# The V slice of a graph-attention layer: two score blocks side by side, and another order of its fifteen products

## The chip, the cores and the metric

The kernel runs on one NeuronCore of a Trainium2 chip. Times are device microseconds of that core: the median of several runs for a verdict, and one profiled execution for everything that is read out of a trace. TensorE is called PE here, and its weight loads PEld; VectorE is DVE, ScalarE is ACT, GpSimd is POOL, SyncE is SP, which only issues transfers. PE writes its results to PSUM; DVE and ACT read them from there; POOL works on SBUF alone.

## The reference, cut to what matters

One layer of masked attention over a graph, with a normalisation and a ReLU ahead of it. `x` is 128 graphs x 128 nodes x 768 features, `adj` 128 x 128 x 128, twelve heads of 64, all in float32.

```python
h = jnp.maximum(_layernorm(x, axis=-1), 0.0)
q = _split_heads(h @ Wq + bq)
k = _split_heads(h @ Wk + bk)
v = _split_heads(h @ Wv + bv)
scores = jnp.einsum('bhqd,bhkd->bhqk', q, k) / jnp.sqrt(HD)
scores = scores + beta * adj_e
scores = jnp.where(adj_e > 0, scores, -9000000000000000.0)
out = jnp.einsum('bhqk,bhkd->bhqd', jax.nn.softmax(scores, axis=-1), v)
x = x + out.transpose(0, 2, 1, 3).reshape(x.shape)
```

## The kernel before, in words

Four graphs make a group `G`; there are 32 groups. Group 0 takes a plain path; groups 1 to 31 run three slices each: `qk0` (Q and K of the first half of the heads), `v` (V of all heads) and `qk1` (Q and K of the second half).

**Products.** In a slice the multiplication of the activations by the weights is done with fifteen products in place of eighteen, at two levels of a scheme of Strassen's kind (`PRODUCTS`, with sums of operands made beforehand). A product (`product_z`, line 531) is 14 matmuls in seven zones, 28 rows in a trace, since each float32 matmul stands there twice, with a weight load each. Each product belongs to one of four chains, `a` to `d`. A chain owns a pair of PSUM banks, from its first product in the slice to its last, and its products add up there: after each product the sum so far is read out and added to or subtracted from one of six results (`uses`), and only then may the chain's next product write to the pair. So the next product of a chain waits for the reading of the one before. In the V slice a first reading of a result is a DVE instruction (line 561, with the bias) and then an ACT instruction (line 562); each later one is one DVE addition (line 571).

**Order.** The tuple `ORDER[slice]` gives the order of the products. A place in it is called a slot here. What stands at slots 0 to 14 of the V slice, with the chain of each, is `1a 0c 3b 5a 2c 7b 10a 6c 11b 13a 4d 9c 14b 8d 12c`. `run` (line 807) issues, for each slot, the matmuls of the product, then what is listed behind it (`behind_product`, line 797: masks of score blocks from the slot before, then the `todo` of this slot, then what fell due), then the readings of this product, then the trailing ACT work, then the `"post"` entries. `then(n, f, ...)` enters `f` at slot `n`. All engines carry out what they are given in that order; nothing is moved by a scheduler after that (`manual_schedule`).

**Score blocks.** `scores(G, u, j)` (line 617) takes a pair of PSUM banks and issues 16 matmuls on 64 x 64 tiles of the array (32 rows of line 626), where products and the weighting with V use 128 x 64 tiles. Then it gives back two of the eight homes (SBUF tiles in which the results of slices lie), those of (0, j) and (1, j); the first reading of a later result takes the home that has been free longest. At the next slot DVE adds the mask (line 634), which frees the PSUM pair, and ACT takes the exponential (line 636). Three score blocks of a group stand in its V slice (u = 0: j = 2 at slot 0, j = 1 at slot 2, j = 0 at slot 7), three in the `qk0` slice of the next group.

**PSUM.** There are four pairs, handed round in the order in which they were given back. In the V slice chains a, c and b hold three, and the fourth goes to a score block, then to chain d, which starts at slot 10.

**Decoding.** When the last product of a result has been read, POOL turns its zones into plain Q, K or V (`decode`, line 581: lines 589 to 592 for Q and K, 600 to 604 for V). A score block needs the decoded results of its columns.

**Other work in the V slice.** For the group after next, ACT takes the statistics of four rows of x in three instructions each (`row_stats`, lines 417 to 419) at posts 1, 5 and 10, and SP loads the next row (line 409) at posts 2 and 6. For the next group ACT normalises x (`norm`, line 446) at posts 3, 4, 7 and 8, two instructions each; DVE transposes it; POOL makes inner sums (lines 469 to 471). DVE adds the results of the attention of the group before (line 708). Weights of a product that are not resident are loaded by SP into a ring of five tiles (`load_T`, line 335), each as soon as a buffer is free.

## Time and profile before

| what | value |
| --- | --- |
| median of three runs | 2707.47 us (2703.18 to 2716.2) |
| the profiled execution's own time | 2712.82 us |
| span of its trace | 2711.0 us |
| granted PE clock, mean | 0.996 |
| PE busy | 99% of the span |
| DVE, POOL, ACT busy | 81%, 77%, 65% |

A matmul's end is modelled in the trace, and one starts while the one before still runs. So the busy share of PE says little, and what counts is when the first matmul of a product starts and when the first of the next one does. A row of the timeline has its start and its length in us, the engine, the line, what it writes and reads, and how many instructions were merged; in square brackets is the idle time of the engine ahead of it and what ended that. A row of the table of waits has the waiting engine and line, what it waited for, and the total, the number and the longest of these waits.

### The profile page before, as it was taken

To read this page: it belongs to the slowest core of one execution; us is meant where nothing else is said; L and a number is where in the kernel's file an instruction comes from. 1 tells how busy PE (TensorE), PEld (TensorE's weight loads), DVE (VectorE), ACT (ScalarE), POOL (GpSimd) and SP (SyncE) were. 2 spreads that over 40 slices of the span, in tenths; PEclk is the share of its full clock that TensorE was granted. 3 is DMA by queue.
4 is the path that set the end of the run, shared out by engine and by line. 5 is a ranking of instruction groups with operands and counts; after the bars stand their busy time and mean duration, and the time that the engine had idled before them with its cause. 6 is when DMAs were issued, how large, how long until landed. Compare 5 with 4: busy or idle time off the path is not lost.

```text
span 2711.0 us, 121562 instructions
## 1 busy us (share of the span) xinstructions
PE 2674.2 (99%) x52029; PEld 2568.3 (95%) x52029; DVE 2188.4 (81%) x2705; ACT 1762.5 (65%) x4612; POOL 2096.0 (77%) x3034
## 2 busy tenths in 40 slices
PE   8999999999999999999999999999999999999997
PEld 7799999999999999999999999999999999999997
DVE  6878888788888788888788878788887888877885
ACT  2476666677666677666767666776666776667653
POOL 4867878777878877888778787778787778887783
PEclk9999999999999999999999999999999999999999
DMA  8789889899889898889899889898898988888875
GB/s 229 262 260 278 274 271 274 259 281 276 271 264 281 260 287 272 271 278 277 259 277 276 275 274 268 269 273 269 270 283 260 280 272 269 280 269 256 253 235 158
DMA packets 530342, 721.73 MB, mean 266 GB/s; under 512 B 105980, under 2 KB 374024, under 8 KB 529800
## 3 DMA queue, kind: packets, MB, share of 16 engines
q1 hardware_dynamic: 528640, 713.12, 86.4%
q8 instruction: 412, 6.75, 1.0%
q10 hardware_dynamic: 1160, 0.79, 0.1%
q14 instruction: 130, 1.06, 0.1%
HBM read 647.73 MB, written 66.05 MB: 263 GB/s over the span
## 4 chain that ended last, share of the span: by engine, by line
PE 87%; POOL 4%; DVE 3%; ACT 2%; DMA 1%; issue 1%; POOLq 0%; DVEq 0%; ACTq 0%
PE pair L547 74%; PE pair L626 7%; PE pair L683 6%; DMA sbig<-in_x_dram 1%; DVE home L571 1%; POOL home L590 1%; POOL home L589 1%; POOL home L592 1%; ACT sbig L419 0%; POOL home L591 0%; ACT sbig L417 0%; ACT home L562 0%; DVE e L634 0%; DVE prep_v L304 0%; ACT e L636 0%
## 5 line engine op out<-in xcount | busy, mean ns | idle before, releaser
L571 DVE TENSOR_TENSOR home<-home,pair 128x896 f32<-128x896 f32 x810 | 860.2, 1075 | 234.2 <-PE pair L547 130.4
L547 PE MATMUL pair<-sbig,T_qk 128*64 128x128 f32 x13888 | 888.6, 274 | 4.1 <-ACT e L666 3.1
L547 PEld LDWEIGHTS pair<-sbig,T_qk 128*64 128x64 f32 x13888 | 758.0, 137 | 17.8 <-issue 8.0
L666 ACT ACTIVATE e<-e,sm 128x64 f32<-128x64 f32 x1512 | 382.2, 341 | 123.5 <-DVE sm L654 123.2
L547 PE MATMUL pair<-A,T_qk 128*64 128x128 f32 x6076 | 415.1, 273 | 0.0
L547 PE MATMUL pair<-T_v,sbig 128*64 128x128 f32 x6944 | 414.2, 274 | 0.3 <-ACT home L562 0.3
L589 POOL TENSOR_TENSOR home<-home 128x256 f32<-128x256 f32 x297 | 227.2, 765 | 237.0 <-DVE home L571 237.0
L683 PE MATMUL pair<-v,e 128*64 128x65 f32 x6048 | 401.8, 221 | 0.0
L565 ACT ACTIVATE home<-pair 128x640 f32<-128x640 f32 x325 | 229.2, 705 | 261.5 <-PE pair L547 196.8
L547 PEld LDWEIGHTS pair<-T_v,sbig 128*64 128x64 f32 x6944 | 385.4, 137 | 6.3 <-issue 4.3
L683 PEld LDWEIGHTS pair<-v,e 128*64 128x64 f32 x6048 | 359.5, 137 | 3.6 <-DVE e L634 0.3
L547 PEld LDWEIGHTS pair<-A,T_qk 128*64 128x64 f32 x6076 | 331.7, 137 | 5.5 <-issue 5.5
L634 DVE SCALAR_TENSOR_TENSOR e<-pair,biasT 128x1024 f32<-128x1024 f32 x189 | 230.4, 1219 | 82.1 <-PE pair L626 82.0
L592 POOL TENSOR_TENSOR home<-home 128x256 f32<-128x256 f32 x297 | 276.3, 930 | 23.3
L590 POOL TENSOR_TENSOR home<-home 128x256 f32<-128x256 f32 x297 | 250.1, 842 | 23.3
L636 ACT ACTIVATE e<-e 128x1024 f32<-128x1024 f32 x189 | 200.2, 1059 | 64.7 <-DVE e L634 56.7
L446 ACT ACTIVATE x<-x,block 128x192 f32<-128x192 f32 x480 | 231.7, 540 | 0.0
L692 ACT ACTIVATE sm<-pair,tiny 128x8 f32<-128x8 f32 x189 | 49.3, 261 | 261.6 <-PE pair L683 261.6
L591 POOL TENSOR_TENSOR home<-home 128x128 f32<-128x128 f32 x297 | 196.9, 663 | 23.3
L547 PE MATMUL pair<-sbig,res_qk 128*64 128x128 f32 x3472 | 211.9, 273 | 0.0
L567 ACT ACTIVATE home<-pair,bqk 128x128 f32<-128x128 f32 x650 | 203.6, 374 | 0.0
L626 PE MATMUL pair<-home 64*64 64x128 f32 x5312 | 196.2, 277 | 6.3 <-issue 4.8
(192 smaller groups left out, 4699.9 us busy)
## 6 DMA issues: line engine op xcount, KB each, us to landing
T_qk<-kept_qk SPq DMA_DIRECT2D x713, 448.0 KB, 4.8
T_v<-kept_v SPq DMA_DIRECT2D x341, 448.0 KB, 4.9
xo<-in_x_dram SPq DMA_DIRECT2D x189, 256.0 KB, 4.5
out_dram<-xo SPq DMA_DIRECT2D x189, 256.0 KB, 5.9
x<-in_x_dram SPq DMA_DIRECT2D x248, 192.0 KB, 6.6
sbig<-in_x_dram SPq DMA_DIRECT2D x116, 384.0 KB, 6.5
kept_qk<-prep_qk SPq DMA_DIRECT2D x23, 448.0 KB, 2.9
adj<-in_adj_dram SPq DMA_DIRECT2D x128, 64.0 KB, 3.9
```

The lines of the kernel that those rows point to most:

```text
L446: nc.scalar.activation(t, t, AF.Relu, bias=shift[G, n], scale=rstd[G, n])
L547: nc.tensor.matmul(p[q:q + HD, at, :], lhs[:, q:q + HD], rhs, start=(first and at % 4 == 0), stop=True, skip_group_check=True)
L565: nc.scalar.activation(t[:, 0:5], p[:, 0:5], AF.Copy, scale=float(sign))
L567: nc.scalar.activation(t[:, at], p[:, at], AF.Identity, bias=bqk[:, of, oc:oc + 1], scale=float(sign))
L571: nc.vector.tensor_tensor(t, t, p[:, 0:7], op)
L589: e.tensor_tensor(t[:, 1:4:2], t[:, 1:4:2], twice(5), ALU.add)
L590: e.tensor_tensor(t[:, 2:5:2], t[:, 2:5:2], twice(1), ALU.add)
L592: e.tensor_tensor(t[:, 0:7:6], t[:, 0:7:6], twice(2), ALU.add)
L626: nc.tensor.matmul(ps[k:k + HD, i, g * N:(g + 1) * N], keys[r, k:k + HD], queries[r], start=True, stop=True)
L634: nc.vector.scalar_tensor_tensor(e, ps, SCORE_CAP * ISCALE, bias, op0=ALU.min, op1=ALU.add)
L666: nc.scalar.activation(o[:, r, b, 0:HD], pa[:, r, b, 0:HD], AF.Copy, scale=t[:, 1, r, b:b + 1])
L683: nc.tensor.matmul(pa[q:q + HD, 2 * g + i, :], k[:, q:q + HD], vt[G, "v", r, h // 4][:, 4 * g + h % 4, :], start=True, stop=True, skip_gro ...
```

## The change

The V slice gets an order of its own, the score block of j = 2 moves from slot 0 to slot 2, ahead of that of j = 1, and two of the four normalisations move one slot up. The order of slots 0 to 14 becomes `1a 0c 5a 2c 3b 10a 7b 6c 13a 11b 4d 9c 14b 8d 12c`; slots 10 to 14 are as before. `row_stats` and the loads of rows keep their slots. The slots whose weights are resident stay the same (1, 5, 10 and 14 of the V slice), but other products stand there.

```diff
-ORDER = {"qk0": ZORDER, "v": ZORDER, "qk1": QORDER}
+PORDER = (1, 0, 5, 2, 3, 10, 7, 6, 13, 11, 4, 9, 14, 8, 12)
+ORDER = {"qk0": ZORDER, "v": PORDER, "qk1": QORDER}
...
         todo.clear()
-        then(0, scores, G, 0, 2)
+        then(2, scores, G, 0, 2)
         then(2, scores, G, 0, 1)
         then(7, scores, G, 0, 0)
         if more:
             then((11, "post"), add_raw, G + 1)
-            for n, at in enumerate((3, 4, 7, 8)):
+            for n, at in enumerate((3, 4, 6, 7)):
                 then((at, "post"), norm, G + 1, 2 + n // 2, n % 2 * 2, n % 2 * 2 + 2)
```

## The prediction

> **What bounds the kernel now.** I read the page first, then the waits, then PE's timeline in V slices with and without stops.

> ```profile
> span 2711.0 us, 121562 instructions
> PE 2674.2 (99%) x52029; PEld 2568.3 (95%) x52029; DVE 2188.4 (81%) x2705; ACT 1762.5 (65%) x4612; POOL 2096.0 (77%) x3034
> ```

> PE bounds it: idle time is 36.8 us of 2711.0. A change that leaves its matmuls alone can gain in two ways only: fewer costs between matmuls, which the trace counts as busy, or fewer stops. Both are seen in the V slice of group 28, here PE alone.

> ```profile
> 2382.79 1.70 PE L547 MATMUL pair<-T_v,sbig 128*64 128x128 f32 x28
> 2384.41 1.10 PE L626 MATMUL pair<-home 64*64 64x128 f32 x32
> 2385.45 1.75 PE L547 MATMUL pair<-res_v,sbig 128*64 128x128 f32 x28
> 2387.03 1.70 PE L547 MATMUL pair<-T_v,sbig 128*64 128x128 f32 x28
> 2388.66 0.67 PE L626 MATMUL pair<-sbig 64*64 64x128 f32 x16
> 2389.14 0.60 PE L626 MATMUL pair<-home 64*64 64x128 f32 x10
> 2390.77 0.44 PE L626 MATMUL pair<-home 64*64 64x128 f32 x6 [1.03 <-issue]
> 2391.14 3.28 PE L547 MATMUL pair<-T_v,sbig 128*64 128x128 f32 x56
> 2394.25 1.70 PE L547 MATMUL pair<-res_v,sbig 128*64 128x128 f32 x28
> ```

> Slot 0, the block of j = 2, slots 1 and 2, the block of j = 1, then slots 3, 4 and 5. From 2391.14 to 2394.25 are two products and a first restart. The second block stops with 26 of its 32 rows done. What that is worth shows beside the slices of groups 10 and 18 (stretches in us, PE busy first, clock and DMA share last):

> ```profile
> 903.80:930.30 26.50, 26.50 (x522) 25.47 (x518) 18.56 (x23) 18.34 (x40) 21.79 (x37) 1.00 0.97 278
> 2382.80:2410.70 27.90, 26.87 (x520) 25.60 (x518) 18.68 (x23) 18.37 (x40) 21.76 (x37) 1.00 0.95 269
> 1559.00:1586.30 27.30, 26.80 (x520) 25.40 (x518) 18.48 (x23) 18.52 (x40) 21.27 (x36) 1.00 0.92 270
> ```

> Group 10 runs its slice without a stop in 26.50 us; group 28 loses 1.4, group 18 loses 0.8. Over the kernel the stops are these:

> ```profile
> PE pair L626 <- issue: 6.5, 8, 1.9
> PEld pair L626 <- POOL home L592: 7.5, 26, 1.3
> PEld pair L547 <- DVE e L634: 4.0, 6, 0.8
> ```

> **The change, part by part.** *Switches.* The built program has the two blocks next to each other on PE behind slot 2. Product to block is 2384.41 - 2382.79 = 1.62 us, block to product 2385.45 - 2384.41 = 1.04, and the product behind it 2387.03 - 2385.45 = 1.58. A product without neighbours of another shape takes 1.53:

> ```profile
> 1002.79 1.70 PE L547 MATMUL pair<-T_v,sbig 128*64 128x128 f32 x28
> 1004.31 1.70 PE L547 MATMUL pair<-res_v,A 128*64 128x128 f32 x28
> 1005.84 3.23 PE L547 MATMUL pair<-T_v,sbig 128*64 128x128 f32 x56
> ```

> (1005.84 - 1002.79 = 3.05 for two.) A block alone therefore costs 1.62 + 1.04 + 1.58 - 2 x 1.53 = 1.18 us. Its matmuls are cheaper: 32 rows last 1.10 and 16 last 0.67, so 16 more cost 0.43 and a block attached to another 2 x 0.43 = 0.86 to 0.87. The change saves 1.18 - 0.87 = 0.31 in each of 31 groups: -9.6. The rows leave it little room (0.27 to 0.33: 8.4 to 10.2), unless the 0.31 isn't the price of the switch; that is a rival below.

> *Slot 2 waits for slot 0.* 5a follows 1a on chain a with one product between them, where there were two and a block. What reads 1a:

> ```profile
> 2384.61 0.41 DVE L561 TENSOR_TENSOR home<-bv_b,pair 128x256 f32<-128x256 f32 x1
> 2385.06 0.71 ACT L562 ACTIVATE home<-pair 128x640 f32<-128x640 f32 x1 [0.39 <-DVE home L561]
> ```

> ACT ends at 2385.77, which is 2.98 us behind the start of 1a. 5a would start 2 x 1.53 = 3.06 behind it, its weight load 0.11 sooner (PEld 1002.68 against PE 1002.79, below), so the load is late. A product that starts together with its first load costs 1.58 in place of 1.53. I take +0.03 a group, +0.9; the bounds are 0 (the load hides) and 0.1 a group, 3 us.

> ```profile
> 1002.68 1.56 PEld L547 LDWEIGHTS pair<-T_v,sbig 128*64 128x64 f32 x28
> ```

> *Slot 6 waits for slot 4.* 7b follows 3b on chain b in the same way; 3b has one reading, on DVE, as has 3b at slot 2 today:

> ```profile
> 2388.84 1.09 DVE L571 TENSOR_TENSOR home<-home,pair 128x896 f32<-128x896 f32 x1 [0.17 <-PE pair L547]
> 2385.66 1.23 DVE L634 SCALAR_TENSOR_TENSOR e<-pair,biasT 128x1024 f32<-128x1024 f32 x1 [0.63 <-PE pair L626]
> 2387.65 1.02 DVE L708 TENSOR_TENSOR xo<-xo,e 128x512 f32<-128x512 f32 x1
> ```

> It ends 2389.93 - 2387.03 = 2.90 us behind the start of 3b, and 7b's first load would start at 3.06 - 0.11 = 2.95. So it costs nothing as long as DVE is free by then, and whatever DVE is late is paid in full. Between the end of the first block and that reading DVE has two masks and one first reading, 2 x 1.23 + 0.42 = 2.9; PE has the second block, 2c and 3b, 0.87 + 0.2 + 1.58 + 1.53 + 0.3 = 4.5. That leaves 1.6 us. The addition of 1.02 stands at slot 2 ahead of the first reading of 5a, and falls into the time of 5a. The first reading of 5a takes the home that the first block frees, so it waits until half of that block is through, some 0.5 us; DVE would then wait for the first mask's block anyway. Cost 0; bounds 0 and, should a whole mask stand in the way, 1.23 a group.

> *PSUM pairs.* 3b takes the pair that the first mask frees, two products earlier in the queue: 1.23 of mask against 0.87 + 0.2 + 1.58 of PE. Hidden.

> *ACT.* Its work in the slice is the same, 18.4 of 26.5 us in the rows of stretches. The exponential of the first block falls later, behind the first reading of 2c. The first reading of 10a moves to slot 5, ahead of the row statistics of post 5, where it stands behind them at slot 6 today. That matters for the stops at slot 10, here in group 18:

> ```profile
> 1573.39 0.84 ACT L417 ACTIVATE sbig<-sbig 128x768 f32<-128x768 f32 x1 [1.16 <-DMA sbig<-in_x_dram]
> 1575.53 0.68 ACT L562 ACTIVATE home<-pair 128x640 f32<-128x640 f32 x1
> 1576.25 1.09 DVE L571 TENSOR_TENSOR home<-home,pair 128x896 f32<-128x896 f32 x1 [3.45 <-ACT home L562]
> 1577.25 1.22 DVE L634 SCALAR_TENSOR_TENSOR e<-pair,biasT 128x1024 f32<-128x1024 f32 x1
> 1578.53 1.74 PE L547 MATMUL pair<-res_v,A 128*64 128x128 f32 x27 [0.50 <-DVE e L634]
> ```

> A row of x lands 1.16 us late; the statistics hold up the first reading of 10a, that the addition of 6c on DVE, that the mask of j = 0 behind it, and that the pair for 4d. With the reading ahead of the statistics this chain is cut: the 4.0 us of six waits go. Bounds 0 (another ACT item is late there) and 5 with the restarts. What is late next is the first reading of 13a, behind the same statistics and two normalisations; its reader on DVE comes with 4d, two slots later, so about 1.5 us of lateness stay covered. The moved normalisations are four ACT instructions of 0.49; their DVE transpose stands at slot 10, so they only get earlier.

> *SP.* No transfer is added. The load of a row waits for statistics that now end some 2 us sooner, so SP is blocked for less; weights for the product at slot 2 were asked for before the slice starts and are needed 1.2 us sooner than now.

> *The stop inside the second block.* Nothing names its releaser ("issue"), and the eight waits of 6.5 us, with what the modelled ends hide (1.29 against 1.03 in group 28), make up some 8 to 9. I take it for instructions that have not arrived:

> ```profile
> q8 instruction: 412, 6.75, 1.0%
> 2377.83 2.29 SPq L189 DMA_DIRECT2D x<-in_x_dram  x4
> x<-in_x_dram SPq DMA_DIRECT2D x248, 192.0 KB, 6.6
> L626 PEldq EVENT_SEMAPHORE  x152: 51/51/51, 161.2 to 2638.4; - x152
> ```

> 412 packets for 2 x 52029 instructions of PE are one for some 250. Where a border between packets falls shows in groups 4, 21 and 29, whose second block stops after 14, 22 and 26 rows:

> ```profile
> 414.32 0.66 PE L626 MATMUL pair<-sbig 64*64 64x128 f32 x14
> 1812.73 0.88 PE L626 MATMUL pair<-home 64*64 64x128 f32 x22
> 2471.87 1.08 PE L626 MATMUL pair<-home 64*64 64x128 f32 x26
> ```

> So it walks half a row a group. Four transfers of x start 5 us ahead of the slice and take 6.6; a packet asked for then comes late. The built program has 1200 waiting-only instructions on PE in place of 1262, two a group fewer (a block's first wait needs one semaphore where it needed two). With a weight load to each row that is one row more: 1.5 a group. From about group 13 on the border then lies behind the block (0.027 us a row) in 2c (0.055 a row), and PE comes to it later. Against that, the second block starts 0.26 us sooner in each group. Bounds: all of it goes (-9), or each of the 31 groups stops for the mean of 6.5 / 8 = 0.8 (+25 - 9 = +16). I take half, -4.5 to -5, being nearer to the walk that the counts show.

> **The sum.** Against the profiled execution (2711.0 of span, 2712.8 in all): -9.6 + 0.9 - 4 - 5 = -17.7, 2695.1. That execution lies 5.35 above the median of 2707.5, and the two last terms hang on late transfers, which differ from run to run; in the median run I give them 7 in place of 9: 2707.5 - 9.6 + 0.9 - 7 = 2691.8. **Forecast: 2692 us.**

> **The rivals.** *A: the stops stay or move.* Late packets and late rows strike another place of the slice; only the switches are saved. For it: DMA is busy 0.92 to 0.97 of each of the three stretches. Against: the cut chain on ACT is plain in the order. 2707.5 - 9.6 + 0.9 = 2699.

> *B: the double block outruns the instructions, slower.* Two blocks, 64 rows in 1.95 us, use them up at 0.03 us a row against 0.055 in products. If every group stops there for 0.8 where eight did: 2707.5 - 8.7 - 2 + 25 - 7 = 2715. It decides from a mean stop of about 0.5 a group on. Against: before the border the slice has the same instructions as now, in 0.3 us less. [...]

> *C: DVE is late for 3b, slower.* One mask in the way of the reading at slot 4, in each group: 31 x 1.23 = 38, 2707.5 - 8.7 + 38 = 2737. It decides from 1.6 us of DVE backlog plus 0.3 on. Against: DVE idles 8 us of each slice in the rows of stretches.

> *D: it isn't the switch.* The 0.31 belongs to each block's own start (its waits, its first loads), and a block behind a block pays it again: 2707.5 + 0.9 - 7 = 2701.

> **Chances.** Forecast 0.60 (2686 to 2698), A 0.22, D 0.05, B 0.08, C 0.05. Half a per cent, about what a measurement of this kernel can tell from no change, is 13.5 us, so the border is at 2694. Three quarters of the forecast's 0.60 lie below it (0.45), and 0.01 of A: faster 0.46. Slower takes C and a quarter of B: 0.07. The rest is 0.47. The range, 2684 to 2705, takes in A and D; outside are C, B and some 0.05 of the forecast's edges.

> **What would show it.** Right: 64 rows of the score line in one run of about 1.97 us behind slot 2, clean slices of group 10 at some 26.2 us; no wait of line 547 for the mask at slot 10; fewer "issue" waits of the block and those of late groups inside 2c. Wrong: more than 0.1 us a group of waits of line 547 for line 562 (slot 2) or line 571 (slot 6), "issue" waits in more than eight groups, or a second block that again costs 1.18.

## The result, and the profile after

| | before | changed |
| --- | --- | --- |
| median, first set of runs | 2709.2 us (7 runs, 2703.18 to 2716.2) | 2695.3 us (7 runs, 2687.78 to 2698.28) |
| ratio there | | 0.9942, 95% interval 0.9928 to 0.9956 |
| median, second set | 2708.13 us (24 runs) | 2695.77 us (7 runs) |
| ratio there | | 0.9953, interval 0.9937 to 0.997 |
| the profiled execution | 2712.82 us | 2689.49 us |

The change saves about half a per cent. Line numbers from `PORDER` on are one higher than before (547 becomes 548, 626 becomes 627, 634 becomes 635). The page of the changed kernel:

```profile
span 2687.6 us, 121530 instructions
PE 2656.0 (99%) x52029; PEld 2563.8 (95%) x52029; DVE 2170.1 (81%) x2705; ACT 1765.9 (66%) x4612; POOL 2103.4 (78%) x3034
```

PE has the same 52029 matmuls and is 18.2 us less busy, though nothing was taken from it. Half of that, 9.0 us, is the cost between matmuls in the V slices, which the trace counts as busy; 3.7 lie in V slices that stop, where a row's modelled end covers the first part of a stop, and 5.5 outside the V slices. PE's timeline in the V slice of group 9, which has no stop, shows the cost between matmuls:

```profile
812.27 1.70 PE L548 MATMUL pair<-T_v,sbig 128*64 128x128 f32 x28
813.79 1.70 PE L548 MATMUL pair<-res_v,sbig 128*64 128x128 f32 x28
815.32 1.72 PE L548 MATMUL pair<-T_v,sbig 128*64 128x128 f32 x28
816.98 1.98 PE L627 MATMUL pair<-home 64*64 64x128 f32 x64
818.88 3.28 PE L548 MATMUL pair<-T_v,sbig 128*64 128x128 f32 x56
821.99 1.70 PE L548 MATMUL pair<-res_v,sbig 128*64 128x128 f32 x28
```

Slots 0, 1 and 2, both blocks as one run of 64 rows, then slots 3 and 4 (56 rows), and slot 5. From the start of slot 2 to that of slot 5 are 821.99 - 815.32 = 6.67 us; three plain products take 3 x 1.53 = 4.59, so two blocks cost 2.08 where they cost 2 x 1.18 = 2.36. The third row lasts 1.72 in place of 1.70: that is 5a behind 1a, which starts 0.02 us behind its first weight load, where slots 0 and 1 start some 0.11 behind theirs. The whole slice, as a stretch:

```profile
812.30:838.50 26.20, 26.20 (x522) 25.47 (x519) 18.19 (x23) 18.37 (x40) 22.06 (x37) 1.00 0.93 279
```

I measure a slice from the start of its first product to that of the next slice's first. The shortest V slice is 26.480 us before and 26.191 after, so an undisturbed group saves 0.289 us, with the wait at slot 2 in it. What V slices have above the shortest I call their excess:

| trace | sum of 31 V slices, us | 31 x the shortest | excess |
| --- | --- | --- | --- |
| before | 839.9 | 820.9 | 19.0 |
| changed | 822.6 | 811.9 | 10.7 |
| changed, second profile | 828.7 | 811.9 | 16.8 |

Between the first two traces the spans differ by 23.4 us: 9.0 from the clean slices, 8.3 from excess, 4.1 in `qk0` (half of it one stop in group 1), 1.8 ahead of group 1. The second profile of the same kernel has 6.1 us more excess, so the 8.3 is partly chance. PE's waits of the changed kernel:

```profile
PE pair L627 <- issue: 3.8, 5, 1.1
PE pair L548 <- issue: 1.5, 4, 0.5
```

The six waits of the product line for the mask are gone; no row of line 548 for line 635 is left. The waits without a releaser remain. In group 1, in the second block:

```profile
161.49 1.53 PE L627 MATMUL pair<-home 64*64 64x128 f32 x45
164.12 0.32 PE L627 MATMUL pair<-home 64*64 64x128 f32 x2 [1.11 <-issue]
```

And in group 14, at the first row of 2c:

```profile
1226.37 1.98 PE L627 MATMUL pair<-home 64*64 64x128 f32 x64
1229.13 2.12 PE L548 MATMUL pair<-T_v,sbig 128*64 128x128 f32 x35 [0.78 <-ACT home L563]
```

The second is put down to an ACT reading, but it stands where the others' walk leads. Counted in PE's matmul rows from the group's first (V starts at 612, the blocks at 696 and 728, 2c at 760), the stops are at 741, 744, 747, 755, 756, 760, 763, 766, 778, 781 and 783 in groups 1, 3, 5, 10, 11, 14, 16, 18, 26, 28 and 29. That is 1.5 rows a group. Before, they were at 740 to 754 in groups 1 to 29: half a row.

What PE waits for there can be read from the traces, which keep the time of each 16 KB packet of instructions (queue q8: 412 packets for 105298 instructions of PE in the kernel before, one for 256). The V slices of all traces of this document have 107 stops of over 0.25 us without a releaser. All of them, and the one in group 14, stand at the same place in PE's count of instructions, 193 or 194 behind a multiple of 256, and PE goes on 1.2 to 1.7 us behind the end of a packet. In the changed kernel's first profile the packet of a group that stops starts 3.4 to 4.5 us after PE has passed the border before; where no stop of over 0.25 us follows, 1.1 to 3.2 us. The packet itself takes about 1.1 us in both, so it starts late and is not slow.

### The profile page after: what moved, and what is told of

Same layout as the page of the kernel before. It is cut to its first block, busy times and chain, and to the rows that moved or that the text cites. A ratio compares the mean times of both kernels' runs of the same rounds, so it can differ in the third digit from the quotient of the medians.

```text
span 2687.6 us, 121530 instructions
## 1 busy us (share of the span) xinstructions
PE 2656.0 (99%) x52029; PEld 2563.8 (95%) x52029; DVE 2170.1 (81%) x2705; ACT 1765.9 (66%) x4612; POOL 2103.4 (78%) x3034
## 4 chain that ended last, share of the span: by engine, by line
PE 93%; DVE 2%; POOL 1%; ACT 1%; issue 1%; DMA 0%; SPq 0%; POOLq 0%; DVEq 0%; ACTq 0%
PE pair L548 80%; PE pair L627 7%; PE pair L684 6%; DVE home L572 0%; ACT e L667 0%; DVE prep_v L305 0%; POOL A L470 0%; POOL prep_qk L288 0%; DVE sbig L465 0%; POOL prep_qk L287 0%; POOL rstd L393 0%; DMA kept_qk<-prep_qk 0%; ACT o_last L667 0%; DMA kept_v<-prep_v 0%; POOL A L471 0%
## 5 line engine op out<-in xcount | busy, mean ns | idle before, releaser
L592 POOL TENSOR_TENSOR home<-home 128x128 f32<-128x128 f32 x297 | 202.7, 683 | 23.3
L470 POOL TENSOR_TENSOR A<-A 128x256 f32<-128x256 f32 x186 | 169.9, 914 | 56.5 <-DVE A L460 56.5
## 6 DMA issues: line engine op xcount, KB each, us to landing
x<-in_x_dram SPq DMA_DIRECT2D x248, 192.0 KB, 6.8
```

Source lines behind the costliest of these rows:

```text
L592: e.tensor_tensor(t[:, 4], t[:, 4], t[:, 6], ALU.add)
```

## The experiments

All ratios are to the kernel before, run on the same chip.

### The order of the products alone

```diff
-        then(2, scores, G, 0, 2)
+        then(0, scores, G, 0, 2)
```

The changed kernel with the block of j = 2 back at slot 0.

> The changed kernel with the block of j = 2 back at slot 0: new order of the products and moved normalisations, but no two blocks side by side. Theory (a switch of tile shape costs 0.31 us, the order cuts the chain of waits to slot 10): a slice without stops takes 26.5 us again, no wait of line 548 for the mask at slot 10, time 31 x 0.3 = 9 us above the changed kernel, about 2704, 3 to 5 us below before. Rival D (the 0.31 belongs to each block's own start): a clean slice stays at 26.2 and the time at that of the changed kernel, 2695. Rival A (nothing but the switches was gained): 2709, the time before.

It was run again beside the second set of runs of the changed kernel:

> The changed order of products with the score block of j = 2 left at slot 0, once more, in the same call as the changed kernel. My theory (two blocks side by side save 0.286 us a group in the clean slice and cost nothing elsewhere but the stops): 8 to 9 us above the changed kernel, as the clean slices are, less what the stops differ by; so 3 to 11 above it. Rival (what the blocks save is given back in longer stops, so that only the order of products helps): within 3 us of the changed kernel, as the first run's medians had it (2698.5 against 2695.3).

Measured: 2698.53 us, ratio 0.9956 (0.9942 to 0.997), and 2701.74, ratio 0.9978 (0.9966 to 0.9989); 3.2 and 6.0 above the changed kernel (the first from another set of runs than the changed kernel's, the second from the same one). The first is less than the 9 that I expected. The shortest V slice is 26.480 and 26.479, as before. So the 0.289 belongs to the pair of blocks side by side and not to the order. That the price is one of the tile shape, and not of any change of work on PE, is borne out by the weighting with V (line 684 of the changed kernel), which has the tiles of the products and stands between the zones of a product:

```profile
846.58 0.28 PE L684 MATMUL pair<-v,e 128*64 128x65 f32 x4
846.70 0.39 PE L548 MATMUL pair<-sbig,T_qk 128*64 128x128 f32 x4
846.92 0.28 PE L684 MATMUL pair<-v,e 128*64 128x65 f32 x4
847.03 1.70 PE L548 MATMUL pair<-sbig,res_qk 128*64 128x128 f32 x28
848.56 1.70 PE L548 MATMUL pair<-sbig,T_qk 128*64 128x128 f32 x28
```

Four rows of a product take 846.92 - 846.70 = 0.22 us there, 0.055 a row as in a plain product, and the product behind them 848.56 - 847.03 = 1.53. No run changes the tile shape of a block alone, so the shape is the likely reason and not a tested one. The waits of the product line for the mask are gone already with the order alone. In medians the pair is worth less than the 8.9 of the clean slices, though. In the V slices of the two pairs of traces it was 830.6 - 822.6 = 8.0 and 828.0 - 828.7 = -0.7: once all of it, once nothing.

### The statistics one slot later, in the kernel before

```diff
-                for g, at in ((1, 1), (2, 5), (3, 10)):
+                for g, at in ((1, 1), (2, 6), (3, 10)):
```

> The kernel before, with the statistics of its third row one slot later (post 6 in place of post 5, the load of the next row with it), so that the first reading of 10a stands ahead of them on ACT, as in the changed kernel; the order of products and of the score blocks is as before. My theory (the six waits of line 547 for the mask at slot 10 come from late statistics ahead of that reading): they go (before: 4.0 us, 6 times), 4 us less in the V slices' slot 10, and the rest of the slice keeps its clean length of 26.48; 2705 beside 2709 for the kernel before. Rival (the waits come from where the masks of the blocks stand in DVE's order): they stay at some 4 us, 2709. If the later statistics delay the normalisations behind them, or the readings of 13a, waits of line 547 for line 562 appear and it is 2710 or more.

Measured: 2700.35 us, ratio 0.9968 (0.9955 to 0.9981). Its waits for the mask:

```profile
PEld pair L626 <- DVE e L634: 0.4, 1, 0.4
```

Line 547 has none. Group 18, which stopped at slot 10 before, runs through; these are slots 9 and 10, 1.52 us apart:

```profile
1572.10 1.70 PE L547 MATMUL pair<-T_v,sbig 128*64 128x128 f32 x28
1573.62 1.70 PE L547 MATMUL pair<-res_v,A 128*64 128x128 f32 x28
```

The cause of these waits is confirmed: the first reading of 10a has to stand ahead of the statistics on ACT. The gain is 8 us where I expected 4; excess fell from 19.0 to 827.9 - 820.9 = 7.0. Of these 12.0 us, 6.4 lie behind slot 3, where nothing is lost any more. The rest are smaller stops in the second block and the product behind it, still at rows 740 to 753. Whether these come from the row of x that is loaded one slot later or are chance stays open.

### The same row statistics one slot earlier, in the changed kernel

```diff
-                for g, at in ((1, 1), (2, 5), (3, 10)):
+                for g, at in ((1, 1), (2, 4), (3, 10)):
```

> The changed kernel with the statistics of the second row at post 4 in place of post 5, so that they stand ahead of the first reading of 10a on ACT again, as before the change. Theory (the stops at slot 10 came from late rows of x ahead of that reading): PE waits for line 563 or for the mask again in some six groups, and as 13a comes one slot sooner here than before, at slot 8 too: +4 to +12 us, 2699 to 2707. Rival (the new order alone took these stops away, the place of the statistics has no part in it): no waits at slots 8 and 10, 2695.

Measured: 2710.49 us, ratio 1.0017 (1.0005 to 1.0028). The whole gain is gone, and the time is above the 2699 to 2707 that I expected. The product line now waits in nearly every group:

```profile
PEld pair L548 <- ACT home L563: 20.9, 28, 1.1
PE pair L548 <- ACT home L563: 13.5, 24, 0.6
```

The stop is not at the mask but at 13a, slot 8, which waits for the reading of 10a: 0.63 us in each of 29 groups, so ACT's order can cost more than the six waits showed.

### The border of packets moved

```diff
-WARM = 13
+WARM = 45
...
-        nc.tensor.matmul(warm[:, 0, 0:P], ident, ident, start=True, stop=True)
+        nc.tensor.matmul(warm[:, 0, 0:36], ident, ident[:, 0:36], start=True, stop=True)
```

64 more rows of PE ahead of everything, so every border between instruction packets falls 64 rows sooner in each group.

> The changed kernel with 45 short warm-up matmuls (36 columns) in place of 13 long ones (128 columns): the same time at the start, but 32 matmuls more, which are 64 rows with 64 weight loads, half an instruction packet, so that every border between packets falls half a packet (64 rows) earlier in each group. Theory (the stops in the second block and in 2c are a packet that lands late behind the transfers of x): these stops, some 10 us in all 31 V slices together, leave the second block and 2c and mostly vanish, time 2685 to 2690. Rival (the stops are a wait for POOL's decoding or another semaphore, tied to the matmul): they stay where they are, 2695. Rival A (the stops only move): as many us of stops at other slots, 2695.

Measured: 2701.08 us, ratio 0.9973 (0.9959 to 0.9986), with a start that is 15.8 us later in the profiled execution (at 2709.98 the slowest of seven). The excess is 823.9 - 811.9 = 12.0, but none of it lies in rows 741 to 783. But for two at row 668, where 5a waits for ACT's reading of 1a, the stops are at rows 679 to 710, at the next border (804 to 830) and, once, at the one after it (956). Group 21, in the first block:

```profile
1816.54 0.65 PE L627 MATMUL pair<-home 64*64 64x128 f32 x11
1818.48 1.75 PE L627 MATMUL pair<-home 64*64 64x128 f32 x53 [1.29 <-issue]
```

A wait for POOL's homes would have stayed at the second block. These stops follow the count of instructions, and here too PE goes on 1.4 to 1.6 us behind the end of a packet. That the stops would vanish was wrong: they moved.

### The transfers of x, moved and spread

Four transfers of 192 KB of x leave SP 5 us ahead of the V slice. First all four behind slot 1 of the V slice:

```diff
-            then((12, "post"), load_x, G + 1, 1)
...
+            then((1, "post"), load_x, G + 1, 1)
```

> The changed kernel with the second load of x for the next group at post 1 of the V slice in place of post 12 of qk0, some 7 us later. Theory (packets of instructions land late behind these four transfers): the packet for the border in the second block is asked for before them, so the stops in the second block and in 2c go, 8 to 10 us less, 2686; should x now be late for the normalisations, ACT shows waits for DMA x at line 447 and part of the gain goes back. Rival (the four transfers have no part in the stops): stops as before, 2695.

Measured: 2690.99 us, ratio 0.9934 (0.9919 to 0.9948). Slot 2 and its blocks stop in no group. Group 5, at slot 7:

```profile
499.59 0.27 PE L548 MATMUL pair<-T_v,A 128*64 128x128 f32 x1
500.52 1.75 PE L548 MATMUL pair<-T_v,A 128*64 128x128 f32 x27 [0.65 <-issue]
```

That is row 873, where it was row 747 in the changed kernel: 126 rows on, the next border. The excess is 824.8 - 811.9 = 12.9, so the 8 to 10 us that I expected were not gained. x is late for ACT as well, 16.0 us in 13 waits of line 447, and in groups 10, 16, 18 and 26 product 13a at slot 8 waits for ACT, 0.4 to 0.6 us each. Then one at a time, from post 8 on:

```diff
-            then((12, "post"), load_x, G + 1, 1)
+            then((8, "post"), load_quarter, G + 1, 1, 0)
+            then((10, "post"), load_quarter, G + 1, 1, 1)
+            then((12, "post"), load_quarter, G + 1, 1, 2)
...
+            then((0, "post"), load_quarter, G + 1, 1, 3)
```

> The changed kernel with the four transfers of 192 KB of the later half of x given out one at a time, at posts 8, 10 and 12 of qk0 and post 0 of the V slice, in place of four together at post 12 of qk0. My theory (instruction packets asked for near the start of the V slice come late because four transfers of x are in the queues together): stops in the second block and in the product behind it shrink from 10 us to some 3 in the trace, with no wait of the normalisations at post 3 for the last quarter; the V slices lose 5 us or more against the changed kernel, about 2689 (2685 to 2693). Rival 1: the packet is late whatever is in the queues beside it, because the mean load of the DMA engines is 0.9: stops stay at 10 us at the same rows, 2695. Rival 2: the stops move to another border, as when the transfers were moved as a whole: 13 us of stops at rows outside 728 to 788, 2693 to 2697. If the last quarter lands too late for the first normalisation at post 3, ACT waits there and the masks of slot 10 wait again: over 2697.

Measured: 2739.3 us, ratio 1.0105 (1.0086 to 1.0125), far above every case that I had named. ACT did wait for x (13.4 us in 16 waits), but no mask at slot 10 was late for it. The waits of SP, then of PE (its lines are six higher, and line 190 is a quarter of x):

```profile
SPq L190 <- DVE A L466: 221.9, 30, 7.8
...
SPq L190 <- DMA T_v<-kept_v: 46.2, 29, 2.3
```

```profile
PE pair L554 <- DMA T_v<-kept_v: 30.7, 30, 2.0
PEld pair L554 <- ACT home L569: 27.1, 21, 2.3
```

The first quarter needs a buffer that DVE's transposes (line 466 here) still read. It stands at the head of SP's queue for 221.9 / 30 = 7.4 us a group, and the weights of the V slice behind it come late: 30 waits of PE, 26 of them at slot 2. So the place was moved back:

```diff
+            then((12, "post"), load_quarter, G + 1, 1, 0)
+            then((14, "post"), load_quarter, G + 1, 1, 1)
...
+            then((0, "post"), load_quarter, G + 1, 1, 2)
+            then((1, "post"), load_quarter, G + 1, 1, 3)
```

> The changed kernel with the four transfers of the later half of x given out one at a time again, now none sooner than in the changed kernel: posts 12 and 14 of qk0, posts 0 and 1 of the V slice. My theory (spreading them from post 8 lost because the first stood in SP's queue for 7 us a group, for the buffer, with the weights of V behind it): no SP wait of the x transfers for DVE beyond the changed kernel's few us, no waits for weights of V, and stops in the second block and in the product behind it smaller than the 10 to 16 us of the two profiles of the changed kernel; 2690 (2686 to 2695), below the changed kernel. Rival 1 (a single transfer delays a packet as four do, or later borders stop instead): 13 us of stops in V slices, 2693 to 2697. Rival 2 (spreading as such costs, since more transfers of x lie beside those of weights): waits for weights of V again, 2705 or more.

Measured: 2685.71 us, ratio 0.993 (0.9913 to 0.9946), excess 816.9 - 811.9 = 5.0. What is left stands at the later border, as in group 5:

```profile
501.79 0.27 PE L554 MATMUL pair<-T_v,A 128*64 128x128 f32 x1
503.06 1.75 PE L554 MATMUL pair<-T_v,A 128*64 128x128 f32 x27 [1.00 <-issue]
```

And once more:

> The changed kernel with the four transfers of the later half of x at posts 12 and 14 of qk0 and 0 and 1 of the V slice, once more: its ratio to the kernel before was 0.993 (0.9911 to 0.9946), the changed kernel's 0.9942 and 0.9953, and the intervals overlap. My theory (spread transfers cut the stops in V slices from 10 to 16 us to some 5): ratio 0.9915 to 0.994 again, stops of 3 to 8 us in V slices, none of over 0.3 us in the second block or in 2c. Rival (the first profile was a lucky one): stops of 10 us or more, ratio 0.9945 to 0.996.

Measured: 2688.58 us, ratio 0.9931 (0.9915 to 0.9947), excess 820.2 - 811.9 = 8.3. Two stops of over 1 us were in 2c again (groups 20 and 27), which the expectation excluded. Twice below the changed kernel's ratios, with intervals that still overlap: some 0.15% better, likely but not settled. It is the fastest version that computes the reference.

### Without the late transfers of x

```diff
     def load_x(G, r):
+        if r and G > 2:
+            xp[G, 1], xg[G, 2], xg[G, 3] = xp[G, 0], xg[G, 0], xg[G, 1]
+            return
         home_x(G, r)
```

> The changed kernel without the transfers of the later half of x from group 3 on (the two graphs of that half are taken from the earlier half's buffer, normalised twice; 0.75 MB less a group to load). My theory (stops at packet borders near the second block come from packets that those four transfers delay): stops in the second block and 2c fall from 10 to 16 us to under 3 us in the trace, V slices at their clean 26.2 us, 2683 (2679 to 2687). Rival (the packets are late behind the weights' transfers, which stay): stops at the same rows in the same number of groups, 2692 or more.

> The changed order with the score block of j = 2 left at slot 0, and without the same transfers of the later half of x. With the transfers, this order alone stood 3.2 and 6.0 us above the changed kernel, where the clean slices differ by 0.286 x 31 = 8.9. My theory (in a group that stops at a border behind the blocks, PE arrives 0.286 us sooner at the same late packet and gives the saving back; some 11 to 14 groups do): without late packets the whole 8 to 9.5 us stand between this run and the changed kernel without those transfers, 2692 beside 2683. Rival (the two blocks side by side cost something elsewhere that the V slices don't show): 3 to 6 us again.

From group 3 on, both kernels leave out these four transfers and use the other two graphs' x in their place, so they show the time only and do not compute the reference. Measured: 2681.18 us, ratio 0.9917 (0.9901 to 0.9933), with the blocks side by side; 2688.57, ratio 0.9942 (0.9926 to 0.9957), with the order alone. A whole V slice of each, the first with the pair, the second without:

```profile
2116.50:2142.69 26.19, 26.19 (x520) 25.46 (x518) 18.26 (x23) 18.41 (x40) 22.04 (x37) 1.00 0.84 260
```

```profile
2123.20:2149.68 26.48, 26.48 (x521) 25.45 (x519) 18.72 (x23) 18.30 (x40) 21.89 (x37) 1.00 0.86 256
```

The DMA share was 0.93 in group 9 of the changed kernel; without the late transfers it is 0.87 in that group. With the pair one stop is left, in group 1, whose transfers are still made:

```profile
PE pair L630 <- issue: 1.8, 1, 1.8
```

In groups 2 to 31 no V slice stops in either kernel. So the late packets are due to these transfers. That there is less traffic in all may have a part in it, but where the same transfers were only moved (above), the stops moved with them. The weights, which are loaded as before, stop no V slice by themselves. Beside group 1, the V slices of the two sum to 816.0 - 30.1 = 785.9 and 820.9 - 26.5 = 794.4: 8.5 us, 0.283 a group, and the medians differ by 7.4. With the transfers it was 3.2 and 6.0.

### The changed kernel again

> The changed kernel once more, beside the other runs of this call, for a second profile and a narrower comparison. My theory: clean V slices of 26.19 to 26.20 us, no wait of line 548 for the mask at slot 10 over 1 us in all, stops in the second block and in 2c at the same rows within one or two (741 in group 1 to 783 in group 29), since the place is set by the count of instructions and not by the run; their sum anywhere from 7 to 14 us; 2693 to 2697. Rival (the places are chance): stops at other rows or in other groups altogether.

Measured: 2695.77 us, stops at rows 741 to 759 in nine of the groups 1 to 13 and at 774 to 783 in five of the groups 23 to 29, and two more at rows 626 and 650. Of these fourteen groups, nine did not stop in the first profile, but where one does, the row is the walk's. The place is fixed by the program; whether a packet is late there depends on the run. The blocks and 2c (rows 696 to 788) lost 15.1 us, a little more than the 14 that I had allowed:

```profile
PE pair L627 <- issue: 6.7, 7, 1.9
PE pair L548 <- issue: 3.3, 5, 1.2
```

## Why the prediction was right, and where it was off

**Switches: right.** The pair of blocks was to save 0.31, less 0.03 for slot 2, in each group; a clean slice saves 0.289. The order alone saves nothing in a clean slice, so the rival that the price belongs to each block's own start falls.

**Slot 2 and slot 6: right.** The row of 5a lasts 0.02 longer, and no wait of line 548 for line 572 appears at slot 6. DVE's 1.6 us of room held.

**Waits for the mask: right in cause, a little too small.** They went in every version in which the reading of 10a precedes the statistics, the kernel before with that one edit among them, and statistics ahead of that reading in the changed kernel cost 0.6 us a group at 13a. I had put 4 us and at most 5. Behind slot 3 the V slices lost 6.4 us before, 3.9 of it at slot 10, and 0.6 after. The single edit brought 0.32% where the rows said 0.15%, but in its trace nearly half of what the V slices gained is smaller stops in the second block, which differ by as much from trace to trace.

**The stop inside the second block: the term that was mis-sized.** The walk of 1.5 rows a group from the count of waiting-only instructions (the traces have 62 fewer) came out to the row, and late groups stop in 2c, as said. But that PE would come to that border later, and so stop less, was not borne out: over rows 696 to 788 the V slices lost 9.7 and 15.1 us in the two profiles, against 12.5 before, where I had counted 8 to 9. I had put down a gain of 4.5 to 5, some 3 in the median; the traces give 2.8 in one and a loss of 2.6 in the other. In the seven traces with the transfers of x in their old place and the border in these rows it is 6.2 to 15.1, so the gain that I forecast is smaller than what one trace differs from the next by. Two things were overlooked. A border that has walked into 2c still meets late packets (rows 760 to 783, in six of the groups 14 to 29 of the first profile). And where a packet is late, its arrival sets when PE goes on, 1.2 to 1.7 us behind the packet's end: what PE saved just ahead of it is lost there. 11 groups in one profile and 14 in the other are 11 x 0.289 = 3.2 to 14 x 0.289 = 4.0 us given back, about what lies between 2691.8 and 2695.3. The runs without the late transfers speak for this (8.5 us of V slices, 7.4 in medians, and every run with the pair below every run without it), but the runs with transfers spread by as much as the effect; it is the likeliest account, not a settled one.

**Luck in the sum.** In the second profile, the nearer one to the median, the span is 18.9 us shorter than before, where the sum said 17.7. That is partly luck. The stops in the second block and 2c gave -2.6 in place of 5, the waits behind slot 3 gave 5.8 in place of 4, and 7.7 in `qk0` and ahead of group 1 stood in no term; why these are shorter is open.

**The rivals.** That stops stay or move was half right: they did both, but the waits at slot 10 went, and the time lies midway between its 2699 and the forecast's 2692. That the double block by itself outruns the instructions is refuted: without the late x, 64 rows in 1.98 us stop in none of 30 groups. It does leave a packet less time: in a group without stops PE is at the border 6.03 us after the one before it in the kernel before (group 9), and 5.52 in the changed one. The prediction took a packet for some 250 instructions; the runs show 256, with borders 126 rows apart, each row with a weight load. At each of the eleven stops of over 0.25 us in V slices of the changed kernel's first profile, one packet starts between the border before and the stop, and PE goes on 1.2 to 1.5 us behind its end: PE waits for that one. Without the late transfers of x no V slice of groups 2 to 31 waited for one. How many packets PE holds ahead of its work, no run shows. A mask in the way of 3b did not appear. One sign that I had set for "wrong" did: waits without a releaser in more than eight groups, nine in one profile and eleven in the other.

## What to carry to other kernels

Two blocks of another tile shape side by side saved one pair of switches here, 0.289 us a group, and a clean slice shows it to the hundredth; read it there, since a median can hide half of it behind late packets (3.2 and 6.0 us of 8.9 here). An order change also changes what stands ahead of what on every other engine: here that was worth some 6 us beside the 9 of the switches, and the kernel before could have had it by moving one entry by one slot. Where a stop has no releaser, count rows to it over the groups: here it walked with the instruction count, 1.5 rows a group in the changed kernel, and followed transfers issued some 10 us before it (from 2377.83 on, ahead of a stop at 2389.7, in group 28 of the kernel before). Look for such transfers and spread them, which gave 2685.71 and 2688.58 us here, but not ahead of the point where their buffer is free: there the queue behind them stood still for 7.4 us a group, and the time was 2739.3.

## What the runs showed of the hardware that was not expected

The first matmuls of the program did not get shorter with fewer columns. PE's first row in the kernel with the border moved, and in the changed kernel:

```profile
1.50 19.42 PE L923 MATMUL pair<-sbig 128*128 128x36 f32 x90 [1.50 <-POOL sbig masks.py:199]
```

```profile
1.50 5.20 PE L923 MATMUL pair<-sbig 128*128 128x128 f32 x26 [1.50 <-POOL sbig masks.py:199]
```

In the changed kernel's trace each of the 26 rows has its own weight load of 128 x 128. The 90 rows of 36 columns take 20.72 - 1.50 = 19.22 us up to the next line's first matmul, 0.214 each. The rows of 128 columns take 0.213 as well, but only from the second (the first takes 0.372) to the 19th; from the 21st on they take 0.112. So fewer columns did not make a row shorter, and a mean of 0.214 has no room for the quicker pace in those 19 us. In the changed kernel's trace the first record of the granted clock, 1.00, starts at 5.80 us, between the starts of the 20th row (5.71) and the 21st (5.86), and nothing is recorded of the rows before, so the cause stays open. I had counted on a third of that time, and the start came 15.8 us later.
